# Convolution stage of a decoder: the order of one turn held by edges, and squares summed on ScalarE

## The chip, the cores and the metric

The kernel runs on one core of a Trainium2 chip, as one launch. A core has a matrix engine (TensorE, PE in the profile; its weight loads are listed as PEld), three engines for elementwise work (VectorE or DVE, ScalarE or ACT, GpSimd or POOL) and a queue engine that issues transfers (SyncE or SP). Each engine works off its own list of instructions in order; an instruction that needs another engine's result waits on a semaphore, and all that stands behind it on the same engine waits with it. The metric is the device time of the launch in microseconds, and lower is better.

## What is computed

The reference is a decoder of four layers with twelve sublayers on 128 x 64 tokens of width 128, each followed by a layer norm. Only the ninth sublayer is touched, `_L2_ffn_ref`; what matters of it:

```
xc  = silu(pointwise(depthwise_conv3(x)))
x1  = x + xc
logits = x1 @ router_w.T + router_b
top_v, top_i = top_k(logits, 2);  top_w = softmax(top_v)
rw  = sum(one_hot(top_i, 8) * top_w)               # 8 experts
ye  = silu(einsum('bsd,eod->bseo', x1, expert_w) + expert_b)
combined = einsum('bse,bseo->bso', rw, ye)
h   = rmsnorm(x1 + combined @ out_w.T + out_b) * norm_w
ff  = gelu(h @ ff_down_w.T + ff_down_b)
out = h + ff @ ff_up_w.T + ff_up_b
x   = layernorm(x + out)
```

## The kernel before

All tokens stay on chip as 16 chunks `X[c]` of 512 tokens (4 tiles of 128 tokens by 128 features). The function `ffn_conv` goes through them in 8 turns of two chunks. Three generators and helpers make up a turn:

- `begin(i)` prepares turn i. For each chunk of the pair it transposes (L1932, `xT_ps`, copied to `xp`), convolves with three matmuls (L1943, `pw_ps`), takes the SiLU on ScalarE (L1945) and adds on GpSimd to give `x1T` in `box` (L1946). Then the router's logits for both chunks (L1951, `lg`), copied to `lgT`, transposed back (L1957, `lgr`), and the top-two weights in 18 small VectorE operations (L1959 and L428 to L475, with one in between on ScalarE, L470). It yields six times: xT, xT, pw, pw, lg, route.
- `units(i, n, t)` is one of eight units of a turn, here g0 to g7. All eight experts for 128 tokens: four matmuls into two PSUM banks (L1975, and L1977 for the bias), two SiLUs on ScalarE (L1979), the product with the routing weights on VectorE (L1980, 128x1024), and three halving adds: L1981 (on GpSimd for odd t, on VectorE for even t), L1982 and L1983 on GpSimd. The results lie in a ring of four buffers.
- `end(i)` finishes turn i: transposes the sums (L1990, `sT`, copied at L1991), multiplies by `out_w` and adds `x1` (L1999 and L2000, `z`), adds the bias on VectorE (L2002, `acc`), squares on ScalarE (L2004), sums on VectorE (L2005), and takes the root in `norm` (L2008, then `rsqrt`, L347 to L352, eleven small VectorE operations in one chain). The same root also serves the layer norm of the turn before: `ln_stats` (L373, L375, L376) gives its variance, and `ln_apply` a scale `lns` (L382) and eight ScalarE operations (L385) that write `X`. Then eight scalings of `acc` (L2016), the transposes `oT` (L332, copied at L339), `with_bias` on GpSimd (L401) and an add of `acc` (L2022), both into `xb`; the small ffn down (L2027, `dn`), its Gelu on ScalarE (L2029, with a table load before it and one after), up (L2035, `u`) and the add (L2037). The yields are: sT, sT, z, z, norm, scaled, oT, oT, dn, u.

The loop at the end of `ffn_conv` says between which units each piece is issued. A scheduler may still move instructions on an engine past each other where nothing forbids it. PSUM has 5 banks for units and others (`wide`) and 3 for all the rest (`bank`); the `r` tiles, which hold `xb`, have 3 buffers, `acc` has 2.

In this version `end` of a turn is spread over the whole of the next one, and its last two pieces (dn, u) are taken in the turn after that (`tail`). `tc.issue_after(ins)` gives every instruction traced in its block an edge behind `ins` if it is on the same engine as `ins`: it fixes an order, and adds no wait.

Of the kernel before, what the change touches and what calls it, by code (L numbers as in the profile page):

```python
# [16 lines left out]
AF = mybir.ActivationFunctionType  # L17
ALU = mybir.AluOpType
AX = mybir.AxisListType
# [6 lines left out]
TPC = 4  # L26
# [214 lines left out]
def tile_decoder(ctx: ExitStack, tc: tile.TileContext, a, out):  # L241
# [9 lines left out]
    mm = nc.tensor.matmul  # L251
# [60 lines left out]
    def row(n):  # L312
        return rows[:, _ROW_AT[n][0] : _ROW_AT[n][1]]
# [54 lines left out]
    def ln_stats(r, v):  # L368

        st = sm.tile([P, TPC, 6], F32, tag="lnst", name="lnst")  # L370
        mv = sm.tile([P, TPC, 2], F32, tag="lnmv", name="lnmv")
        for t in range(TPC):
            V.bn_stats(st[:, t, :], r[:, t, :])  # L373
        for t in range(TPC):
            V.bn_aggr(mv[:, t, :], st[:, t, :])  # L375
        V.tensor_scalar(v, mv[:, :, 1], LN_EPS, None, ALU.add)  # L376
        return mv

    def ln_apply(c, r, mv, y, store=False, on_act=False, on_dve=False):
        if on_act:  # L380
            s = sm.tile([P, TPC], F32, tag="lns", name="lns")
            last = V.scalar_tensor_tensor(s, mv[:, :, 0], -1.0, y, ALU.mult, ALU.mult)  # L382
        for t in range(TPC):
            if on_act:
                A.activation(X[c][:, t, :], r[:, t, :], AF.Identity, bias=s[:, t : t + 1], scale=y[:, t : t + 1])  # L385
            else:
                (V if on_dve else G).tensor_scalar(X[c][:, t, :], r[:, t, :], mv[:, t, 0:1], y[:, t : t + 1], ALU.subtract, ALU.mult)  # L387
        if store:
            nc.sync.dma_start(out=out_v[c], in_=X[c])
        return last if on_act else None  # L390
# [766 lines left out]
    def rows32(t, g):  # L1157
        return t[32 * g : 32 * g + 32]
# [731 lines left out]
    def ffn_conv():  # L1890
# [77 lines left out]
        def units(i, n, t):  # L1968

            s = S_[i]  # L1970
            y = ring[count[0] % 4]
            count[0] += 1
            ps = [wide("ye_ps") for _ in range(2)]
            for k in range(2):
                mm(ps[k].rearrange("p (e d) -> p e d", e=4), s["x1T"][n][:, t * P : (t + 1) * P], w[0][:, 4 * k : 4 * k + 4, :], start=True, stop=False, skip_group_check=True)  # L1975
            for k in range(2):
                mm(ps[k], rows32(ones, k), rows32(be, k)[:, k * 512 : (k + 1) * 512], start=False, stop=True, skip_group_check=True)  # L1977
            for k in range(2):
                s["silu"] = A.activation(y[:, 4 * k : 4 * k + 4, :], ps[k].rearrange("p (e d) -> p e d", e=4), AF.Silu)  # L1979
            V.tensor_tensor(y, y, s["w"][:, n * TPC + t, :, None].to_broadcast([P, E8, D]), ALU.mult)  # L1980
            (G if t % 2 else V).tensor_tensor(y[:, :4], y[:, :4], y[:, 4:], ALU.add)  # L1981
            G.tensor_tensor(y[:, :2], y[:, :2], y[:, 2:4], ALU.add)  # L1982
            G.tensor_tensor(s["sum"][n][:, t * D : (t + 1) * D], y[:, 0], y[:, 1], ALU.add)  # L1983

        def end(i):
            s = S_[i]
            for n in pair:
                ps = bank("sT_ps")
                for t in range(TPC):
                    nc.tensor.transpose(ps[:, t * P : (t + 1) * P], s["sum"][n][:, t * P : (t + 1) * P], ident)  # L1990
                A.copy(s["sumT"][n], ps)  # L1991
                yield
            v = sm.tile([P, 2, 2, TPC], F32, tag="cv", name="cv")
            acc = []
            for n in pair:
                z = bank("z")
                for t in range(TPC):
                    q = slice(t * P, (t + 1) * P)
                    mm(z[:, q], s["x1T"][n][:, q], ident, start=True, stop=False)  # L1999
                    mm(z[:, q], s["sumT"][n][:, q], w[1][:, 1, :], start=False, stop=True)  # L2000
                h = work("o", (P, TPC, D), "acc")
                V.tensor_tensor(h, z.rearrange("p (t d) -> p t d", t=TPC), row("outb")[:, None, :].to_broadcast([P, TPC, D]), ALU.add)  # L2002
                sq_ = work("ye", (P, TPC, D), "sq")
                A.activation(sq_, h, AF.Square)  # L2004
                V.tensor_reduce(v[:, 0, n], sq_, AX.X, ALU.add)  # L2005
                acc.append(h)
                yield
            V.tensor_scalar(v[:, 0], v[:, 0], 1.0 / D, 1e-6, ALU.mult, ALU.add)  # L2008

            y = norm(v, i - 1, S_[i - 1] if i else None)  # L2010
            yield
            hT, base = [], []
            for n in pair:
                h = acc[n]
                for t in range(TPC):
                    V.scalar_tensor_tensor(h[:, t, :], h[:, t, :], y[:, 0, n, t : t + 1], row("normw"), ALU.mult, ALU.mult)  # L2016
            yield
            for n in pair:
                h = acc[n]
                hT.append(transposed(h, "oT"))  # L2020
                b = with_bias(2 * i + n, "upb")
                G.tensor_tensor(b, b, h, ALU.add)  # L2022
                base.append(b)
                yield
            ps = bank("dn_ps")
            for n in pair:
                mm(ps[32 * n : 32 * n + 32, :], col("downw"), hT[n], start=True, stop=True)  # L2027
            g = work("xT", (64, 512), "g32")
            A.activation(g, ps[:64, :], AF.Gelu, bias=col("downb")[:64])  # L2029
            yield  # L2030
            us = [bank("u") for _ in pair]
            for t in range(TPC):
                q = slice(t * P, (t + 1) * P)
                for n in pair:
                    mm(us[n][:, q], rows32(g, n)[:, q], rows32(w[1], n)[:, 2, :], start=True, stop=True)  # L2035
            for n in pair:
                V.tensor_tensor(base[n], us[n].rearrange("p (t d) -> p t d", t=TPC), base[n], ALU.add)  # L2037
            s["r"] = base
            yield

        def norm(v, i, s):
            if s is None:
                G.memset(v[:, 1], 1.0)
            else:
                mv = [ln_stats(s["r"][n], v[:, 1, n]) for n in pair]
            y = rsqrt(v.rearrange("p a n t -> p (a n t)"), 4 * TPC, "rms").rearrange("p (a n t) -> p a n t", a=2, n=2)
            if s is not None:
                for n in pair:
                    ln_apply(2 * i + n, s["r"][n], mv[n], y[:, 1, n], on_act=True)
            return y  # L2050

        def take(it, n=1):
            for _ in range(n):
                next(it, None)
# [1 line left out]
        none = iter(())  # L2056
        first = begin(0)
        take(first, 7)
        tail = none
        for i in range(turns):  # L2060
            b = begin(i + 1) if i + 1 < turns else none
            e = end(i - 1) if i else none
            for g in range(8):
                units(i, g // TPC, g % TPC)
                if g == 0:
                    take(tail)
                    take(b, 2)
                elif g == 1:
                    take(tail)
                    take(e, 2)  # L2070
                elif g == 2:
                    take(b, 2)
                elif g == 3:
                    take(e, 3)
                elif g == 4:
                    take(e)
                elif g == 5:
                    take(b)
                elif g == 6:
                    take(b)  # L2080
                elif g == 7:
                    take(e, 2)
            tail = e
        take(tail, 2)
# [4 lines left out]
        norm(v, turns - 1, S_[turns - 1])  # L2089
        return S_[turns - 1]["silu"].ins  # L2090


# [130 lines left out]
```

## Time and profile before

| | us |
|---|---|
| median of 9 runs | 3190.74 |
| lowest, highest | 3177.69, 3201.59 |
| profiled execution | 3201.5 |
| its span | 3199.7 |
| the convolution's work lies at about | 2134 to 2490 |

In the stretch from 2305 to 2345 us, about one turn, the busy times are: PE 36.15, VectorE 33.63, ScalarE 18.72, GpSimd 24.66 of 40 us, at a mean granted TensorE clock of 0.91; transfers are near nothing. Between 2145 and 2465 us, mean durations of one instruction: L1980 1.313 us (least 1.184), L1979 0.600, L1981 on GpSimd 1.379 and on VectorE 0.769, L1982 0.860, L1983 0.659, L2016 0.605, L1946 1.250, L401 1.368, L2022 1.775, L2004 0.629, L2005 0.682. A mean well above the least duration means that the instruction was held up while it ran.

How to read the views: the chain of work gives the work that ended last, followed back in time; the waits give, for each pair, who stood still until whom; the timeline lists instructions by start, with their length, and in brackets the idle time of the engine before them and what ended it; "x8" at the end means that eight were merged into one line. The windows give the busy time of each engine within a stretch.

### The profile page before, as it was taken

Reading aid. Unit: us, or ns where it says so; the run is one execution under the profiler, and the core shown is the slowest. Engines: PE = TensorE matmul, PEld = TensorE weight load, DVE = VectorE, ACT = ScalarE, POOL = GpSimd, SP = SyncE. Lnnn points to the kernel's source line nnn. Section 1 sums busy time; section 2 is a strip of 40 time slices with the busy share of each in tenths; the row PEclk is TensorE's granted clock in tenths of the full one; section 3 lists DMA queues with packets and bytes.
Section 4 is the critical chain, followed back from the end, with each engine's and each line's share of the span. In section 5 each row is a group of like instructions: output and inputs, shape, how many; then the busy total and the mean of one; then the engine's idle time right before and its main releaser. Section 6 shows DMA issues by size and latency. Waiting matters only on the chain. (4 is left out here: it accounts for less than half of the span.)

```text
span 3199.7 us, 110578 instructions
## 1 busy us (share of the span) xinstructions
PE 2809.2 (88%) x46690; PEld 2058.0 (64%) x46690; DVE 2023.5 (63%) x7300; ACT 1620.9 (51%) x3150; POOL 1534.4 (48%) x1543
## 2 busy tenths in 40 slices
PE   5899989989898999997799989999997679998993
PEld 3789856656666677865577767764433347766882
DVE  3732469667777666553376656667889876674355
ACT  2444468845444555332366555544454556654453
POOL 3566566144554444334277445556665223344344
PEclk9999989999998999898899989989998889997996
DMA  4578821000002000014511000000000000011783
GB/s 127 151 205 259 240 59 43 12 2 3 3 3 63 11 4 4 6 32 114 154 18 18 4 5 4 4 11 1 1 1 10 1 6 18 19 33 54 216 249 112
DMA packets 191633, 182.22 MB, mean 57 GB/s; under 512 B 30176, under 2 KB 166624, under 8 KB 191136
## 3 DMA queue, kind: packets, MB, share of 16 engines
q1 hardware_dynamic: 160688, 136.66, 14.7%
q0 software_dynamic: 20224, 32.28, 4.3%
q8 instruction: 366, 6.00, 0.8%
q10 hardware_dynamic: 10224, 6.22, 0.7%
q14 instruction: 131, 1.07, 0.1%
HBM read 132.34 MB, written 42.73 MB: 55 GB/s over the span
## 5 line engine op out<-in xcount | busy, mean ns | idle before, releaser
L1243 DVE TENSOR_REDUCE m<-s_ps 128x8 f32<-128x512 f32 x640 | 397.2, 682 | 133.1 <-PE s_ps L1602 47.2
L1292 ACT ACTIVATE e<-t_ps 128x512 f32<-128x512 f32 x640 | 329.9, 602 | 158.0 <-PE t_ps L1285 157.4
L1310 PE MATMUL av_ps<-vx,e 128*64 128x18 f32 (+1 forms) x10240 | 344.7, 217 | 8.3 <-issue 7.3
L1310 PEld LDWEIGHTS av_ps<-vx,e 128*64 128x64 f32 x10240 | 325.7, 141 | 29.5 <-issue 22.1
L792 ACT ACTIVATE hT<-h_ps,aux 128x256 f32<-128x256 f32 x496 | 206.8, 469 | 228.4 <-PE h_ps L790 119.3
L1187 POOL TENSOR_SCALAR eb<-qT,small 128x512 f32<-128x512 f32 x80 | 131.4, 1643 | 344.8 <-ACT qT L972 149.7
L1273 PE MATMUL t_ps<-eb,kT 32*64 32x128 f32 x10240 | 282.7, 286 | 6.8 <-DVE m L1243 2.3
L825 POOL DMA_INDIRECT got<-l_rout,fat x192 | 191.9, 1000 | 179.1 <-DVE r L835 70.3
L790 PE MATMUL h_ps<-ebT,rw 128*128 128x256 f32 x992 | 244.6, 391 | 19.0 <-DVE ebT L778 11.0
L803 PEld LDWEIGHTS yg<-rw,hT 128*128 128x128 f32 x1984 | 242.8, 193 | 6.6
L1273 PEld LDWEIGHTS t_ps<-eb,kT 32*64 32x64 f32 x10240 | 199.6, 132 | 73.3 <-DVE m L1243 25.7
L803 PE MATMUL yg<-rw,hT 128*128 128x128 f32 x1984 | 243.0, 276 | 0.0
L1235 PE MATMUL s_ps<-eb,qT 32*64 32x256 f32 x5120 | 219.5, 400 | 18.4 <-POOL eb L1187 9.4
L387 POOL TENSOR_SCALAR x<-xb,lnmv,ln_y 128x128 f32<-128x128 f32 x200 | 157.0, 797 | 160.8 <-DVE ln_y L352 160.8
L1315 DVE RECIPROCAL rc<-av_ps 128x32 f32<-128x32 f32 (+1 forms) x192 | 61.5, 320 | 241.5 <-PE av_ps L1310 241.2
L765 POOL DMA_INDIRECT aux<-in_x_dram,rat x156 | 159.7, 1024 | 113.3 <-PE h_ps L790 48.8
L790 PEld LDWEIGHTS h_ps<-ebT,rw 128*128 128x128 f32 x992 | 183.9, 196 | 45.0 <-DVE ebT L778 15.8
L804 DVE TENSOR_TENSOR yo<-yg,aux 128x256 f32<-128x256 f32 x124 | 52.3, 422 | 243.4 <-PE yg L803 243.2
L1185 ACT ACTIVATE eb<-qT,small 128x512 f32<-128x512 f32 x160 | 106.8, 715 | 128.7 <-POOL qT L1412 123.9
L1187 POOL TENSOR_SCALAR eb<-kT,small 128x512 f32<-128x512 f32 x80 | 144.8, 1810 | 21.5 <-ACT kT L972 11.5
L1235 PEld LDWEIGHTS s_ps<-eb,qT 32*64 32x64 f32 x5120 | 113.9, 134 | 60.8 <-issue 14.5
L1975 PE MATMUL ye_ps<-w_l2f,box 128*128 128x512 f32 x256 | 136.2, 651 | 0.0
(519 smaller groups left out, 6367.4 us busy)
## 6 DMA issues: line engine op xcount, KB each, us to landing
rw<-in_l0w_dram SPq DMA_DIRECT2D x78, 512.0 KB
rw<-in_l3w_dram SPq DMA_DIRECT2D x46, 512.0 KB
l_rout<-yo SPq DMA_DIRECT2D x124, 128.0 KB
aux<-xd SPq DMA_DIRECT2D x46, 128.0 KB
aux<-in_l0b_dram SPq DMA_DIRECT2D x78, 66.0 KB
xd<-vx SPq DMA_DIRECT2D x5, 1024.0 KB
plan<-xr ACTq DMA_DIRECT2D x18, 256.0 KB
x<-in_x_dram SPq DMA_DIRECT2D x16, 256.0 KB
```

Source lines behind the costliest of these rows:

```text
L387: (V if on_dve else G).tensor_scalar(X[c][:, t, :], r[:, t, :], mv[:, t, 0:1], y[:, t : t + 1], ALU.subtract, ALU.mult)
L765: s.gather = G.indirect_dma_start(out=eb[:, i, :], out_offset=None, in_=x[:, :], in_offset=bass.IndirectOffsetOnAxis(ap=at[:, i : i + 1], ...
L790: s.pe = mm(ps[:, j * GR : (j + 1) * GR], w1[:, (k + j) * P : (k + j + 1) * P], ebT, start=True, stop=True)
L792: s.act_ins = A.activation(hT[k + j], ps[:, j * GR : (j + 1) * GR], s.act, bias=v[:, k + j : k + j + 1])
L803: s.pe = mm(y[:, i * P : (i + 1) * P], hT[k][:, i * P : (i + 1) * P], w2[:, k, :], start=(k == 0), stop=(k == FK - 1))
L825: s.gather = G.indirect_dma_start(out=got[i][k][:, t, :], out_offset=None, in_=s.rout[b][:, :], in_offset=bass.IndirectOffsetOnAxis(ap=at[ ...
L1187: ins = (G if h == 2 else V).tensor_scalar(dst, x, mine, None, ALU.mult)
L1235: mm(ps[g][j * S : (j + 1) * S, u * 256 : (u + 1) * 256].rearrange("p (h k) -> p h k", h=4), rows32(s["q"], g)[:, b], rows32(s["eb"], g)[: ...
L1243: last = V.tensor_reduce(s["m"][:, g, 2 * hf : 2 * hf + 2, :].rearrange("p t h -> p (t h)"), ps[g].rearrange("p (n k) -> p n k", k=S), AX. ...
L1273: mm(ps[g][i * S : (i + 1) * S].rearrange("p (a u j q) -> p a u j q", u=2, a=2, j=2)[:, :, u, j, :], rows32(s["k"], g)[:, b], rows32(s["eb ...
L1292: last = A.activation(e[:, g, :], ps[g], AF.Exp, scale=scale)
L1310: mm(av[j * S : (j + 1) * S, 8 * (u - u0) + n, :], ev[:, n // 2, n % 2, u, j, :], vx[:, 2 * (2 * hf + u) + j, n, :], start=True, stop=True,)
```

## The change

Seven things are edited, all in `ffn_conv`:

1. `end`: the square of 128x512 (L2004) and the sum of its rows on VectorE (L2005) become four ScalarE squares of 128x128, each of which also gives the sum of its rows (`accum_out`).
2. `end`: `ln_stats` of the turn before is issued behind each half of `z`, and no longer in `norm`.
3. `end`: the root (`roots`), the eight scalings and then `ln_apply` (`applied`) are one piece, with no yield between them.
4. The loop: the units behind the scaling get an edge behind the last scaling, so that on VectorE no product may come between the root and the scalings.
5. The loop: all pieces get an edge behind the last matmul of the unit before them.
6. The loop: z and root come behind g2 (they were behind g3), the second half of `begin`'s convolution behind g3 (it was behind g2), oT behind g5 (g7), dn behind g6 (g0 of the next turn), u behind g7 (g1 of the next turn).
7. `tail` is gone.

```diff
         def end(i):
...
-                A.activation(sq_, h, AF.Square)
-                V.tensor_reduce(v[:, 0, n], sq_, AX.X, ALU.add)
+                for t in range(TPC):
+                    A.activation(sq_[:, t, :], h[:, t, :], AF.Square, accum_out=v[:, 0, n, t : t + 1])
                 acc.append(h)
+                if i:
+                    mv.append(ln_stats(S_[i - 1]["r"][n], v[:, 1, n]))
                 yield
             V.tensor_scalar(v[:, 0], v[:, 0], 1.0 / D, 1e-6, ALU.mult, ALU.add)
-
-            y = norm(v, i - 1, S_[i - 1] if i else None)
-            yield
-            hT, base = [], []
+            if not i:
+                G.memset(v[:, 1], 1.0)
+            y = roots(v)
             for n in pair:
                 h = acc[n]
                 for t in range(TPC):
-                    V.scalar_tensor_tensor(h[:, t, :], h[:, t, :], y[:, 0, n, t : t + 1], row("normw"), ALU.mult, ALU.mult)
+                    last = V.scalar_tensor_tensor(h[:, t, :], h[:, t, :], y[:, 0, n, t : t + 1], row("normw"), ALU.mult, ALU.mult)
+            s["scaled"] = last.ins
+            if i:
+                applied(i - 1, mv, y)
             yield
...
             for g in range(8):
-                units(i, g // TPC, g % TPC)
...
+                with tc.issue_after(scaled) if scaled else nullcontext():
+                    pe = units(i, g // TPC, g % TPC)
+                with tc.issue_after(pe):
+                    if g == 0:
+                        take(b, 2)
+                    elif g == 1:
+                        take(e, 2)
+                    elif g == 2:
+                        take(e, 3)
+                        scaled = S_[i - 1]["scaled"] if i else None
+                    elif g == 3:
+                        take(b, 2)
+                    elif g == 5:
+                        take(e, 2)
+                        take(b)
+                    elif g == 6:
+                        take(e)
+                        take(b)
+                    elif g == 7:
+                        take(e)
```

The two programs can be built and their lists of instructions compared, engine by engine. For a steady turn of the changed one (turns 2 to 6) the lists are these, with the line numbers of the kernel before:

```
TensorE  g0, xT, g1, sT, g2, z, z, g3, pw, pw, g4, g5, oT, oT, lg, g6, dn, lgr, g7, u
ScalarE  SiLU g2, squares (4, 4), SiLU g3, box (first), L385 x8, box (second),
         SiLU g4, SiLU g5, oT copies, lgT copy, SiLU g6, table load, Gelu, table load, SiLU g7
VectorE  L1980 g2, acc (first), L1981 g2, acc (second), L2008, root (11), scaling (8), lns (2),
         L1980 g3, L1980 g4, L1981 g4, L1980 g5, L1980 g6, L1959, L1981 g6, 11 of routing,
         L2037, 1 of routing, L1980 g7, 2 of routing, L2037, the other 3 with statistics,
         L1980 g0, L1981 g0, statistics, L1980 g1, statistics
GpSimd   L1982 and L1983 g2, L2022 (first), L1946 (first), L1981 g3, L401, L1982 g3,
         L2022 (second), L1983 g3, L401 (for the next turn), L1946 (second),
         then L1982 and L1983 of g4, L1981 to L1983 of g5, and so on to g1
```

In the kernel before, the same piece of GpSimd's list reads: L1946 (first), L1946 (second), then the adds of three units, L2022 (first), L401, L2022 (second), L401 (for the next turn); on TensorE `oT` stands between the first matmuls of the next turn's g0 and g1, and on VectorE products and routing stand between the root's operations. Outside of the convolution stage and its border with the next one, the lists are the same.

More of the change, by code (lines that the diff above doesn't have):

```diff
@@ L1976, in units @@
             for k in range(2):
-                mm(ps[k], rows32(ones, k), rows32(be, k)[:, k * 512 : (k + 1) * 512], start=False, stop=True, skip_group_check=True)
+                pe = mm(ps[k], rows32(ones, k), rows32(be, k)[:, k * 512 : (k + 1) * 512], start=False, stop=True, skip_group_check=True)
             for k in range(2):
@@ L1983, in units @@
             G.tensor_tensor(s["sum"][n][:, t * D : (t + 1) * D], y[:, 0], y[:, 1], ALU.add)
+            return pe.ins
         def end(i):
@@ L1993, in end @@
             v = sm.tile([P, 2, 2, TPC], F32, tag="cv", name="cv")
-            acc = []
+            acc, mv = [], []
             for n in pair:
@@ L2015, in end @@
                 for t in range(TPC):
-                    V.scalar_tensor_tensor(h[:, t, :], h[:, t, :], y[:, 0, n, t : t + 1], row("normw"), ALU.mult, ALU.mult)
+                    last = V.scalar_tensor_tensor(h[:, t, :], h[:, t, :], y[:, 0, n, t : t + 1], row("normw"), ALU.mult, ALU.mult)
+            s["scaled"] = last.ins
+            if i:
+                applied(i - 1, mv, y)
             yield
+            hT, base = [], []
             for n in pair:
@@ L2039, in end, with roots, applied @@
             yield
[L2041 to L2050, printed above, removed]
+        def roots(v):
+            return rsqrt(v.rearrange("p a n t -> p (a n t)"), 4 * TPC, "rms").rearrange("p (a n t) -> p a n t", a=2, n=2)
+        def applied(i, mv, y):
+            for n in pair:
+                ln_apply(2 * i + n, S_[i]["r"][n], mv[n], y[:, 1, n], on_act=True)
         def take(it, n=1):
@@ L2058, in ffn_conv @@
         take(first, 7)
-        tail = none
+        scaled = None
         for i in range(turns):
@@ L2063, in ffn_conv @@
             for g in range(8):
-                units(i, g // TPC, g % TPC)
[L2065 to L2084, printed above, removed]
+                with tc.issue_after(scaled) if scaled else nullcontext():
[18 more added lines that the diff above has]
+                        take(e)
         for _ in end(turns - 1):
@@ L2088, in ffn_conv @@
         G.memset(v[:, 0], 1.0)
-        norm(v, turns - 1, S_[turns - 1])
+        mv = [ln_stats(S_[turns - 1]["r"][n], v[:, 1, n]) for n in pair]
+        applied(turns - 1, mv, roots(v))
         return S_[turns - 1]["silu"].ins
```

## The prediction

> **What bounds the kernel now.** The granted clock and engine shares of the whole span say little here: the change touches one stage. I read first the chain of work that ended last between 2120 and 2520 us, where the convolution stage lies (start, length, engine, tile, line):
>
> ```profile
> 2305.79 5.42 PE pw_ps L1943 x12
> ...
> 2319.98 0.64 ACT sq L2004
> ...
> 2331.69 4.32 DVE acc L2016 x8
> ...
> 2347.96 5.42 PE pw_ps L1943 x12
> ```
>
> The same piece of work comes back every 42.2 us: one turn. The second square of a turn stands in this chain at 2195.62, 2235.64, 2277.80, 2319.98, 2362.15 and 2404.67; the timeline has the seventh at 2439.85. These six periods, 244.2 us, are what the change can alter most; I measure all by this mark (the second `acc` ends just before it).
>
> Second, the waits between 2145 and 2465 us (who waited for whom: total us, times, longest):
>
> ```profile
> PEld oT_ps L332 <- DVE acc L2016: 38.5, 31, 7.1
> PE oT_ps L332 <- DVE acc L2016: 25.6, 17, 6.8
> ACT x L385 <- DVE lns L382: 17.0, 6, 4.5
> PEld lg_ps L1951 <- POOL box L1946: 8.8, 7, 4.3
> ```
>
> TensorE stands before the transposes `oT` until VectorE has scaled: about 3.7 us a turn. The last row is small now: `lg` seldom waits for GpSimd.
>
> Third, the timeline of one turn, 2327.5 to 2349 us. Here VectorE and GpSimd hold each other up:
>
> ```profile
> 2331.61 4.40 DVE L2016 SCALAR_TENSOR_TENSOR acc<-acc,rms_y,rows 128x128 f32<-128x128 f32 x8
> 2331.65 3.19 ACT L385 ACTIVATE x<-xb,lns,rms_y 128x128 f32<-128x128 f32 x8 [2.44 <-DVE lns L382]
> ...
> 2333.02 1.31 POOL L2022 TENSOR_TENSOR xb<-xb,acc 128x512 f32<-128x512 f32 x1 [0.75 <-DVE acc L2016]
> 2334.28 1.31 POOL L401 TENSOR_TENSOR xb<-x,rows 128x512 f32<-128x512 f32 x1
> ...
> 2336.07 1.21 DVE L1980 TENSOR_TENSOR units<-units,route 128x1024 f32<-128x1024 f32 x1
> ...
> 2336.15 2.25 POOL L2022 TENSOR_TENSOR xb<-xb,acc 128x512 f32<-128x512 f32 x1 [0.55 <-DVE route L436]
> ```
>
> The eight scalings need 4.40 us; one alone is 0.34 (the line's minimum is 0.336). The second L2022, caught behind a product L1980, takes 2.25 us where the first took 1.31. So a VectorE operation on two SBUF tiles and a GpSimd operation take turns, and whichever is queued waits out the other.
>
> Fourth, the busy time in 2-us windows (length, PE, PEld, DVE, ACT, POOL, granted clock):
>
> ```profile
> 2333.80:2335.80 2.00, 0.74 (x2) 0.18 (x2) 2.00 (x3) 1.51 (x4) 1.80 (x2) 0.60 0.04 8
> 2335.80:2337.80 2.00, 2.00 (x4) 0.86 (x5) 2.00 (x4) 0.00 (x0) 1.65 (x1) 0.50 0.00 0
> 2337.80:2339.80 2.00, 2.00 (x4) 0.53 (x2) 1.93 (x4) 0.58 (x1) 2.00 (x3) 0.50 0.00 0
> 2339.80:2341.80 2.00, 2.00 (x9) 0.60 (x9) 1.90 (x5) 0.90 (x3) 1.84 (x3) 0.69 0.00 0
> ```
>
> After the stall the clock is at half for some 7 us; with 0.60, 0.50, 0.50 and 0.69 that is 3.4 us of lost matmul time. The stall is thus paid twice, and removing it should bring 5 us a turn, if nothing replaces it.
>
> **The change, part by part, on a steady turn.** Let 0 be the end of the second `acc`. I follow the built order of each engine, in the line numbers of the kernel before, and put measured durations on it.
>
> *Squares.* Two 128x512 squares (0.63) and two VectorE reductions (0.68 each) go; eight 128x128 squares with a sum come. No row shows a sum taken by ScalarE. Bounds for one: 0.17 (L1816, a 128x128 ACTIVATE, 0.275, less the 0.11 by which two SiLUs of 0.597 overlap) and 0.48 (L385, 128x128 with two pointers). I take 0.35, nearer L385, whose pitch is 3.19/8 = 0.40. The last four are on the path: 1.4 us, 0.05 hand-over. The Trainium skill, "ScalarE: Activation LUTs", section "What ACT_TABLE_LOAD costs", gives 186 ns + 0.833 ns an element less about 93 of overlap, which as an estimate is 0.2 each, and the turn 0.6 shorter; it states no price for the sum, and no run here shows one.
>
> *Root and scaling unbroken.* Now they are spread from 2321.4 to 2336.0, 14.6 us, because products and routing lie between. Unbroken, the last turn of this profile shows their price: L347 at 2476.48 to the last L352 at 2478.73 is 2.25 us for 11 operations. Scaling:
>
> ```profile
> 2478.92 3.23 DVE L2016 SCALAR_TENSOR_TENSOR acc<-acc,rms_y,rows 128x128 f32<-128x128 f32 x8
> ```
>
> that is 3.23 beside one GpSimd operation; 4.40 beside three. In the new order two (L2022, L1946) are ready by then: 3.8. With L2008 (0.2) and two `lns` (0.25): 1.45 + 0.2 + 2.3 + 3.8 + 0.25 = 8.0 us. `oT` is then ready before TensorE, which has 13 us of work from `z` to there (g3, `pw` 5.3, g4, g5, at 2.24 a unit, plus `oT` 1.0). The old stall is gone.
>
> *What is queued behind it.* All products from g3 on now stand behind the scaling. On GpSimd the order is: L2022, L1946 (first half), then L1981 of g3, L401, L1982, L2022, L1983, L401, and only then L1946 for the second half, on which `lg` waits; and on TensorE `lg` stands before g6. On ScalarE the eight L385 (3.2 us) wait for `lns`, and behind them stand the second `box` (0.69) and the SiLUs of g4 and g5, so g4's product can't begin before 8.0 + 3.2 + 0.7 + 1.1 = 13 us. GpSimd: product g3 done at 9.25; then 1.27 + 1.26 + 0.73 + 1.30 + 0.46 + 1.26 + 1.19 = 7.5, hand-overs 0.3. VectorE's L1980, L1981, L1980 of g4 and g5 (3.1) arrive in that time and take turns; less 0.15 of overlap each, 2.7. So the second `lg` starts at 9.25 + 7.8 + 2.7 = 19.75 us. TensorE has been there since about 12: a stall of 7 us in place of the 3.7.
>
> *From `lg` on.* `lg` 0.86, g6 1.92, 0.48 to ScalarE, two SiLUs 1.08, 0.05: 4.4 us to the product of g6. After such a stall the clock is at half; bounds for this stretch 0 and 2.8 (all of it); I take 2.5 by the windows above. The skill's "TensorE: Matmul & The Clock Gate", Part 1, states that one busy window of 3.4 us restores full rate, which as an estimate would cost 1.7 instead; the rows above show it at half for longer. Product g6 at 26.65.
>
> VectorE's own queue from there to the next second `acc`: five L1980 at 1.21, three L1981 at 0.61, L1959 0.2, 17 routing operations at 0.25 (their pitch at 2145), two L2037 1.2, eight L373 1.7, eight L375 0.65, two L376 0.3, two `acc` 1.3: 17.5 us bare. GpSimd's 7.3 us for g6, g7, g0 and g1 take turns with it; some 4 show. Bounds: 1.5 (they fall under the operations that don't contend) and 6.9 (the factor of the present turn, from 2336.0 to 2354.1: 18.1 us for 13.0 bare; 17.5 x 0.39). With 4: 21.5. **Period: 26.65 + 21.5 = 48.1 us** against 42.2.
>
> *Ends.* In the first turn that ends another, there are no L385, L401 or statistics yet: so GpSimd's list there is L2022 twice, product g3's L1981 and L1982, then the second L1946: scaled 8.7, L2022 10.0, product g3 11.25, L1981 12.5, one L1980 13.7, L1982 14.4, L1981 15.1, L1946 16.3; with 4.4 + 0.8 (a shorter stall, clock mostly up) + 21.5 the period is 43 (41 to 45) against 40.0. The first mark comes 5.3 us earlier, as `pw` now follows `z`. The small ffn inside its turn removes, at the end, a wait of 4.09 us (`sT` for L2037, at 2467.69), but the last product, now behind the scaling, comes at about 24.6 after the mark instead of 17.4; the sums then take 2.6, so `sT` follows at 27.4 against 27.9: nothing. Cover for that is GpSimd's sum; were it gone, 4 us would be won. No DMA is moved.
>
> Sum: -5.3 + 43 + 5 x 48.1 - 244.2 = **+34 us**. The profiled execution took 3201.5 us (span 3199.7, 1.8 around it), so 3235.5; it lies 10.8 above the median of 3190.74, so on the scale of medians **3225**.
>
> **Rivals.**
> *The stall goes for good* (faster). If GpSimd and VectorE hardly met and the clock stayed up: `lg` at 7.4 + 1.25 + 7.8 = 16.5, product g6 at 20.9, plus 17.5: 38.4 a turn. -5.3 + 39 + 192 - 244.2 = -18.5: 3172; a quarter of the contention and clock loss counted above gives 3185. For it: the waits of `oT` for `acc` do vanish. Against: the L2022 of 2.25 us.
> *TensorE sets the pace* (about even). VectorE keeps up (contention 1.5) and only `lg` stalls: 19.75 + 0.86 + 2.24 + the rest of the turn's matmuls 16.7 + 2.5 + 1.1 for `acc`, 43.2. -5.3 + 41 + 216 - 244.2 = +7.5: 3198. Decides if VectorE reaches the second `acc` when `z` ends.
> *More contention* (slower). 6.9 in place of 4, squares 0.48 each, scaling 4.4: 52.1 a turn, 45 for the first, +56: 3247.
> *The order isn't what it says*: the built orders exclude it, but if ScalarE's sum were a long operation (1 us each), the period grows by 2.6, to 3238.
>
> **How the numbers follow.** About 0.3%, 9.6 us, is what a measurement of this kernel can tell from no change. Forecast 3225 (its own range 3205 to 3245): 0.62; stall gone: 0.13; TensorE's pace: 0.15, of which 0.08 within 0.3%, 0.03 faster and 0.04 slower; more contention and the long sum: 0.10. Faster 0.13 + 0.03 = 0.16, same 0.08, slower 0.62 + 0.04 + 0.10 = 0.76. The range reaches down to a quarter of the contention, 3184, and up to the case of more contention, 3247; about 2 in 10 lie outside.
>
> **What would show it.** Right: the wait of `oT` for `acc` near nothing; a wait of `lg` for L1946 of 5 to 8 us a turn; L347 to the last L352 within 2.5 us; marks about 48 us apart; granted clock at half after `lg`. Wrong: `lg` waiting under 3 us, or marks under 42 us apart: then GpSimd's queue was ready sooner than I count, and the forecast falls with it.

## The result, and the profile after

The changed kernel takes **3211.81 us** (median of 20 runs, 3191.76 to 3224.84); the kernel before, run beside it, 3189.99 (62 runs). The ratio is 1.0073, with a 95% interval of 1.0058 to 1.0087: slower by 19 to 28 us. The profiled execution took 3215.5 us (span 3213.8).

Line numbers are now those of the changed kernel: `acc` L2003, squares L2006, L2011 (was L2008), scaling L2018, the add of `acc` into `xb` L2028, `dn` L2033, Gelu L2035, `u` L2041 and L2043; up to L1983 nothing moved. A turn is measured from mark to mark, the mark being the end of its second `acc`. I cut the stage at three points: the first `pw` weight load, the seventh mark, and the last weight load of `kva`, near the end of the next stage (`attn_scan`), which begins under the convolution's last turns.

| us | before | after | difference | predicted |
|---|---|---|---|---|
| first `pw` to first mark | 64.2 | 57.0 | -7.2 | -5.3 |
| first period | 40.0 | 41.7 | +1.7 | +3 |
| four steady periods | 169.0 | 177.8 | +8.8 | +23.4 |
| sixth period | 35.7 | 44.1 | +8.4 | +12.4 |
| seventh mark to last `kva` | 153.4 | 160.0 | +6.6 | 0 |
| sum | 462.3 | 480.6 | +18.3 | +34 |

The first and the sixth period's rows belong together: `pw` now follows `z`, so every mark but the last ones comes a `pw` earlier, and the kernel before has no `pw` left in its sixth period. Together they make +1.2, and the sixth turn's own loss is in it. A steady turn takes 44.4 us against 42.2. The chain of work that ended last, in the changed kernel, from one mark (2322.82) on (start, length, engine, tile, line):

```profile
2326.94 3.86 DVE acc L2018 x7
2330.94 1.15 DVE units L1980
2332.16 1.27 POOL units L1981
2333.43 1.22 POOL xb L401
...
2336.51 1.45 POOL box L1983
2337.96 1.67 POOL xb L401
2339.63 2.12 POOL box L1946
2341.79 1.92 PE lg_ps L1951 x2
2343.71 3.22 PE ye_ps L1975 x4
...
2348.54 1.23 DVE units L1980
```

Before, this part of the chain was scaling and transposes; now it leads through GpSimd's whole list, add by add, to the second L1946, and only then to `lg` and g6. The waits between 2145 and 2465 us, one row of the kernel before, then the changed kernel's (who waited for whom: total us, times, longest):

```profile
DVE units L1980 <- ACT units L1979: 21.2, 14, 4.1
```

```profile
DVE units L1980 <- ACT units L1979: 68.0, 12, 8.1
...
PE lg_ps L1951 <- POOL box L1946: 40.0, 8, 6.0
...
PE oT_ps L332 <- DVE acc L2018: 1.1, 2, 0.9
```

TensorE's old wait (25.6 us, `oT` for the scalings) is nearly gone (1.1); a wait of 40.0 for GpSimd stands in its place, and VectorE, which waited 21.2 us for SiLUs before, now waits 68.0. The timeline of VectorE in one turn shows where:

```profile
2324.16 0.17 DVE L2011 TENSOR_SCALAR cv<-cv 128x8 f32<-128x8 f32 x1 [1.34 <-ACT sq L2006]
...
2326.67 4.13 DVE L2018 SCALAR_TENSOR_TENSOR acc<-acc,rms_y,rows 128x128 f32<-128x128 f32 x8
...
2335.73 1.92 DVE L1980 TENSOR_TENSOR units<-units,route 128x1024 f32<-128x1024 f32 x1 [3.65 <-ACT units L1979]
...
2348.54 1.23 DVE L1980 TENSOR_TENSOR units<-units,route 128x1024 f32<-128x1024 f32 x1 [7.83 <-ACT units L1979]
```

Three gaps in a turn: 1.34 us for the squares, 3.65 for g4's SiLUs and 7.83 for g6's. In between it is busy without a pause. So the account of a turn is VectorE's: busy time and gaps. The windows view gives it, for one turn of the kernel before and then of the changed one (length, busy time of PE, PEld, DVE, ACT, POOL with instructions, granted clock):

```profile
2319.46:2361.62 42.16, 38.38 (x145) 17.30 (x144) 35.22 (x76) 20.85 (x41) 25.84 (x28) 0.92 0.00 0
```

```profile
2322.82:2367.25 44.43, 36.02 (x145) 16.73 (x144) 30.85 (x74) 22.17 (x55) 25.63 (x29) 0.88 0.00 1
```

VectorE's busy time falls by 4.4 us (35.22 to 30.85), but it stands still for 13.6 us in place of 6.9. The second outweighs the first by 2.3 us a turn.

### The profile page after: what moved, and what is told of

Same layout as the page of the kernel before. It is cut to its first block, busy times and chain, and to the rows that moved or that the text cites. A ratio compares the mean times of both kernels' runs of the same rounds, so it can differ in the third digit from the quotient of the medians.

```text
span 3213.8 us, 110706 instructions
## 1 busy us (share of the span) xinstructions
PE 2790.3 (87%) x46690; PEld 2047.6 (64%) x46690; DVE 1996.5 (62%) x7284; ACT 1634.4 (51%) x3264; POOL 1539.7 (48%) x1543
## 5 line engine op out<-in xcount | busy, mean ns | idle before, releaser
L1310 PE MATMUL av_ps<-vx,e 128*64 128x18 f32 (+1 forms) x10240 | 337.5, 215 | 9.2 <-issue 8.4
L1310 PEld LDWEIGHTS av_ps<-vx,e 128*64 128x64 f32 x10240 | 318.9, 139 | 29.8 <-issue 22.2
L1273 PEld LDWEIGHTS t_ps<-eb,kT 32*64 32x64 f32 x10240 | 198.9, 132 | 73.3 <-DVE m L1243 25.6
L765 POOL DMA_INDIRECT aux<-in_x_dram,rat x156 | 159.9, 1025 | 117.3 <-PE h_ps L790 51.7
L1980 DVE TENSOR_TENSOR units<-units,route 128x1024 f32<-128x1024 f32 x64 | 93.5, 1467 | 68.3 <-ACT units L1979 68.0
```

The lines of the kernel that those rows point to most:

```text
L765: s.gather = G.indirect_dma_start(out=eb[:, i, :], out_offset=None, in_=x[:, :], in_offset=bass.IndirectOffsetOnAxis(ap=at[:, i : i + 1], ...
L1273: mm(ps[g][i * S : (i + 1) * S].rearrange("p (a u j q) -> p a u j q", u=2, a=2, j=2)[:, :, u, j, :], rows32(s["k"], g)[:, b], rows32(s["eb ...
L1310: mm(av[j * S : (j + 1) * S, 8 * (u - u0) + n, :], ev[:, n // 2, n % 2, u, j, :], vx[:, 2 * (2 * hf + u) + j, n, :], start=True, stop=True,)
```

## Experiments

Each row below is one kernel; the times are from its profiled execution, the ratio is to the kernel before, run beside it on the same chip (the kernel before took 3317 us beside e1 and 3186 us beside e11, so only ratios are compared). Where one order is changed, the builder may move other instructions too; what it moved is told with each.

| run | period (mean of the second to fifth), us | first `pw` to 7th mark | 7th mark to last `kva` | ratio, 95% interval |
|---|---|---|---|---|
| before | 42.2 | 308.9 | 153.4 | 1 |
| after | 44.4 | 320.6 | 160.0 | 1.0073 (1.0058 to 1.0087) |
| e1 GpSimd's order | 39.2 | 293.4 | 159.8 | 0.9958 (0.9931 to 0.9985) |
| e2 ScalarE's order | 40.6 | 302.4 | 160.1 | 1.0011 (0.9988 to 1.0035) |
| e3 both | 40.8 | 299.6 | 156.6 | 0.9984 (0.9957 to 1.0010) |
| e4 no edge | 40.5 | 300.0 | 158.7 | 0.9994 (0.9964 to 1.0024) |
| e5 L385 behind Gelu | 44.5 | 315.4 | 146.5 | 1.0000 (0.9973 to 1.0026) |
| e6 last turn | 39.3 | 291.6 | 152.8 | 0.9973 (0.9947 to 0.9999) |
| e7 sums on VectorE | 40.4 | 299.8 | 162.1 | 1.0003 (0.9976 to 1.0031) |
| e8 before, sums on ScalarE | 43.4 | 312.1 | 150.8 | 1.0036 (1.0017 to 1.0055) |
| e9 L385 behind copies | 40.7 | 302.7 | 156.1 | 0.9974 (0.9955 to 0.9993) |
| e10 L385 split | 39.8 | 295.5 | 156.3 | 0.9965 (0.9948 to 0.9981) |
| e11 as e6 | 39.2 | 293.6 | 155.7 | 0.9971 (0.9954 to 0.9987) |
| e12 two adds fewer | 37.4 | 280.8 | 156.8 | 0.9937 (0.9907 to 0.9966) |

A profile is one execution. e6 and e11 are the same kernel twice: from the first `pw` to the first mark they take 54.0 and 56.8 us, from there to the seventh mark 237.6 and 236.7, and from that to the last `kva` 152.8 and 155.7. So the periods can be compared closely, and a difference of 3 us in the first or the last stretch says little.

### e1: the second `x1T` add ahead of the bias adds

The theory to test: GpSimd's order alone makes `lg` late.

```diff
+                s["x1"] = G.tensor_tensor(...x1T...).ins
...
-                b = with_bias(2 * i + n, "upb")
-                G.tensor_tensor(b, b, h, ALU.add)
+                with tc.issue_after(S_[i + 2]["x1"]) if i + 2 < turns else nullcontext():
+                    b = with_bias(2 * i + n, "upb")
+                    G.tensor_tensor(b, b, h, ALU.add)
```

> GpSimd takes the second x1T add (L1946) ahead of both bias adds and both adds of the scaled tile; nothing else moves. Theory (GpSimd's list alone keeps lg waiting): the second lg starts at 13.3 us after the mark (second box done 12.0, add 1.2) instead of 19.0, product g6 at about 20, the stretch to the next mark stays 18.7, period 38.7 instead of 44.4; five steady turns give -28 and the first -3: about 3181 us, ratio to before 0.997. Rival (contention: the four adds now fall beside VectorE's products and routing): stretch 21.5 to 23, period 41.5 to 43, 3195 to 3204. Rival (VectorE alone sets the pace): no gain, 3212.

VectorE's, ScalarE's and TensorE's lists stay as they were; only GpSimd's changes. The period falls from 44.4 to 39.2 us. The timeline of e1, from its mark at 2406.34 (GpSimd, then VectorE):

```profile
2417.15 1.17 POOL L1946 TENSOR_TENSOR box<-xp,box 128x512 f32<-128x512 f32 x1
2418.29 3.93 POOL L401 TENSOR_TENSOR xb<-x,rows 128x512 f32<-128x512 f32 x2
2422.18 4.45 POOL L2029 TENSOR_TENSOR xb<-xb,acc 128x512 f32<-128x512 f32 x2
...
2418.14 1.27 DVE L1980 TENSOR_TENSOR units<-units,route 128x1024 f32<-128x1024 f32 x1 [3.65 <-ACT units L1979]
2419.45 1.64 DVE L1981 TENSOR_TENSOR units<-units 128x512 f32<-128x512 f32 x1
2421.01 4.50 DVE L1980 TENSOR_TENSOR units<-units,route 128x1024 f32<-128x1024 f32 x2
```

L1946 is done 12.0 us after the mark (18.9 in the changed kernel), and the gap of 7.83 us is gone. The product of g6 ends 19.2 us after the mark in place of 26.95, 7.8 us sooner. But the four adds now lie beside products: two L1980 take 4.50 us together, where two undisturbed ones take 2.4 (e.g. 2.35 at 2462.83 in the changed kernel), and from the end of g6's product to the next mark it is 20.0 us in place of 17.5. So 7.8 is won and 2.5 given back: both the theory and the first rival hold in part. VectorE's busy time says the same, 33.38 against 30.85:

```profile
2406.34:2445.47 39.13, 35.68 (x146) 17.02 (x144) 33.38 (x74) 21.93 (x55) 26.91 (x29) 0.96 0.00 1
```

### e12: two GpSimd adds fewer

The disputed cost by itself: e1 with `with_bias` left out, `b = X[c] + h`, so that the bias of the small ffn is missing from its result.

```diff
-                    b = with_bias(2 * i + n, "upb")
-                    G.tensor_tensor(b, b, h, ALU.add)
+                    b = work("r", (P, TPC, D), "xb")
+                    G.tensor_tensor(b, X[2 * i + n], h, ALU.add)
```

> GpSimd's order, and the two bias adds (L401) of a turn left out, so that the small ffn's bias is missing in the result; VectorE, ScalarE and TensorE keep their lists, GpSimd has two adds of 1.22 us fewer. Theory (a VectorE operation on SBUF and a GpSimd operation take turns, so each GpSimd add queued beside VectorE's products lengthens VectorE's work by about its own time): period 39.2 less 2 to 2.5, 36.7 to 37.2, VectorE busy 34.1 to 32 in a turn. Rival (the products are long for another reason): 39.2. Rival (the other adds slide under the same products and half comes back): 38.

```profile
2300.67:2338.09 37.42, 34.20 (x145) 16.34 (x144) 31.67 (x74) 21.94 (x55) 24.36 (x27) 1.00 0.00 1
```

VectorE does the same 74 instructions in 31.67 us in place of 33.38, with the same gaps (1.34 and 3.65); the period falls by 1.7. Two adds of 1.22 us cost VectorE 1.7 us, 0.7 of their own time; expected were 2 to 2.5. Over the four steady turns the busy time falls from 33.46 to 31.66 us: 0.55 of it in the products, 0.81 in the halving adds, 0.49 in the routing, and nothing in root and scaling together. "Take turns" is right, the full price is not. A reason can be read from e1's trace: in its steady turns a product takes between 1.21 and 2.29 us, but L2003, L2044 and L373, which read one tile of SBUF, keep to 0.68, 0.68 and 0.28 us beside GpSimd's adds, so what of an add falls beside those costs nothing. The Trainium skill, "SBUF — State Buffer", section "Who interferes with whom", says that a VectorE instruction with two SBUF inputs contends with a GpSimd instruction that reads SBUF, and that one with at most one SBUF input, outside VectorE's two-port modes, does not; these durations agree.

### e2 and e3: L385 behind the SiLUs of g4 and g5

The other thing that comes late is g4's product (gap of 3.65 us), since its SiLUs stand behind eight L385 on ScalarE.

```diff
-            if i:
-                applied(i - 1, mv, y)
             yield
+            if i:
+                with tc.issue_after(S_[min(i + 1, turns - 1)]["silu"].ins):
+                    applied(i - 1, mv, y)
+            yield
...
                     elif g == 5:
-                        take(e, 2)
+                        take(e, 3)
```

> ScalarE takes the eight L385 behind the second box and the SiLUs of g4 and g5; the builder then also sets the second x1T add ahead of the bias adds on GpSimd. Theory: second lg at 12.6 us after the mark (product g3 9.25, A1 1.3, A2 0.75, add 1.2), and the products of g4 and g5 follow g3 at once (VectorE idle there 0 instead of 3.65); period 37.5 to 38.5, about 3178 us, ratio 0.996. Rival (when g4 and g5 come does not matter, only lg): the same as the run with GpSimd's order alone, 38.7, 3181. Rival (L385 late holds up statistics or buffers): over 41, 3195 or more.

> Both orders together. Theory: as with ScalarE's order alone, since the second x1T add is already early there; 3175 to 3180 us. Rival (bias adds behind the x1T add meet VectorE's products): 3185 to 3195.

e2 is this edit alone (the builder then also sets the second L1946 ahead of L401), e3 has e1's as well. Both beat the changed kernel, 40.6 and 40.8 us, but neither comes near 38, and e3's period is longer than e1's. The timeline of e3, mark at 2386.09:

```profile
2398.04 3.18 ACT L385 ACTIVATE x<-xb,lns,rms_y 128x128 f32<-128x128 f32 x8
2401.12 1.05 ACT L339 COPY oT<-oT_ps 128x512 f32<-128x512 f32 x2
...
2404.30 0.23 DVE L1959 TENSOR_TENSOR route<-lgr_ps,rows 128x64 f32<-128x64 f32 x1 [3.85 <-PE lgr_ps L1957]
```

L385 now stands in front of the `oT` copies; `dn` waits for those, `lgr` stands behind `dn` on TensorE, and L1959, which the builder put ahead of g6's product, waits 3.85 us (4.72 in e2). The gap has moved, not shrunk. Neither theory held; nearest comes e2's last rival (L385 late, over 41 us), but what L385 holds up is `dn` and `lgr`, not statistics or buffers.

### e4: no edge behind the scaling

```diff
-                with tc.issue_after(scaled) if scaled else nullcontext():
+                with nullcontext():
                     pe = units(i, g // TPC, g % TPC)
```

> Products are not held behind the scaling: the edge is left out, one product now stands inside the root, the second box stands ahead of L385 and the second x1T add ahead of the unit adds. Theory (the edge is what makes lg late): root and scaling end 1.3 us later, second lg at 10 to 13 us, oT waits under 1 us, period 38 to 40, 3178 to 3188 us. Rival (scaling early is what pays): oT waits again 3 us a turn and the time is above the changed kernel's, 3215 to 3230.

One product now lies inside the root, and the builder puts the second box ahead of L385 on ScalarE and both L1946 ahead of the bias adds. The scalings take 5.00 us in place of 4.13 and end 11.5 us after the mark in place of 8.0; `oT` waits 7.3 us between the first mark and the seventh, 1.2 us a turn. Yet the period is 40.5, a little above what was expected, and the time at the upper end of it: with the edge left out, and L1946 early, 4 us a turn are back. This does not show that the edge costs them. e1 has L1946 early too, keeps the edge, and its period is 1.3 us shorter than e4's (whose second box also stands elsewhere). So the loss lies in GpSimd's order that came with the edge, not in scaling early.

### e5, e9 and e10: other places for L385

All with e1's order; e9 and e10 also with the last turn of e6, below. e5 puts the eight behind the Gelu, e9 behind the `oT` copies; e10 puts four behind the copies and four behind the Gelu, and holds the statistics of the next turn behind g7's product.

```diff
-            A.activation(g, ps[:64, :], AF.Gelu, bias=col("downb")[:64])
+            gelu = A.activation(g, ps[:64, :], AF.Gelu, bias=col("downb")[:64])
+            if i:
+                with tc.issue_after(gelu.ins):
+                    applied(i - 1, mv, y)
...
+            if i:
+                with tc.issue_after(last_copy[0]):
+                    applied(i - 1, mv, y)
             ps = bank("dn_ps")
```

> GpSimd's order as in the run with GpSimd's order alone, and on ScalarE the second box and the SiLUs of g4 and g5 first, the eight L385 only behind the Gelu, in front of g7's SiLUs. Theory (with GpSimd's order VectorE sets the pace: of its 39.2 us it stands idle 1.34 before L2011 and 3.65 before the product of g4): the 3.65 shrink to about 1.6, period 37 to 37.5, 12 us less than with GpSimd's order alone, ratio to before 0.991 to 0.993. Rival (a late ScalarE chain takes the place, as where L385 stood in front of the oT copies: VectorE idle 3.85 before L1959): period 39 to 41, ratio 0.996 to 0.999.

> GpSimd's order, the last turn's old end, and on ScalarE the second box and the SiLUs of g4 and g5 first, then the oT copies, then the eight L385, in front of g6's SiLUs. Theory (VectorE sets the pace; idle 1.34 before L2011 and 3.65 before g4's product with GpSimd's order alone): 3.65 shrink to 1.7, but g6's SiLUs come up to 3 us later and VectorE waits 1 to 2 there: period 38.2 to 39.5, stage within 6 us of 444. Rival (Gelu and with it u, the statistics and xT come late, as where L385 stood behind the Gelu): 42 to 44.

> As the run with L385 behind the copies, but four L385 there and four behind the Gelu, and VectorE's statistics held behind the product of g7. Theory: neither g6's SiLUs nor g7's product come late; VectorE idle 1.34 plus 1.7 plus under 1; period 37.2 to 38.2, stage 434 to 440, ratio to before 0.991 to 0.993. Rival (the builder's other shifts give it back): 39 to 40, ratio 0.994 to 0.996.

None beats e1's 39.2: 44.5, 40.7 and 39.8. e5 lies above its theory and its rival, e9 (stage 458.8 us) above its theory, e10 in its rival's range. In e5 g7's SiLUs come behind L385, and the builder set its product behind all routing and statistics, 28.6 us after the mark (26.3 in e1). Its sums on GpSimd come late, `sT` waits for them, and with it g2 (VectorE, TensorE, VectorE; mark at 2403.70):

```profile
2432.32 2.35 DVE L1980 TENSOR_TENSOR units<-units,route 128x1024 f32<-128x1024 f32 x2
...
2438.37 0.47 PE L1991 MATMUL sT_ps<-ident,box 128*128 128x128 f32 x1 [4.10 <-POOL box L1983]
...
2444.01 1.23 DVE L1980 TENSOR_TENSOR units<-units,route 128x1024 f32<-128x1024 f32 x1 [4.99 <-ACT units L1979]
```

e10 is the telling one, for there nothing on ScalarE is late any more (mark at 2304.74; in this kernel L1981 are the SiLUs and L1982 the products):

```profile
2314.71 1.36 DVE L1982 TENSOR_TENSOR units<-units,route 128x1024 f32<-128x1024 f32 x1 [1.73 <-ACT units L1981]
...
2321.73 1.58 DVE L1982 TENSOR_TENSOR units<-units,route 128x1024 f32<-128x1024 f32 x1 [2.67 <-ACT units L1981]
...
2320.54 1.08 ACT L1981 ACTIVATE units<-ye_ps 128x512 f32<-128x512 f32 x2 [0.55 <-PE ye_ps L1979]
```

VectorE's gaps are 1.34, 1.73 and 2.67, no less in sum than e1's 1.34 and 3.65, and the SiLUs behind the last one waited for TensorE. TensorE has no gap from the mark until then: `pw` 5.4 us, three units, `oT`, `lg`, up to 2320.4, 15.7 us after the mark. So with L385 out of the way VectorE waits for matmuls in the first half of a turn; e5 has the same two gaps, 1.73 and 2.67, there. e10's mean holds one turn of 41.2 us; its other three take 39.2 to 39.4, e1's period.

### e6 and e11: the border with the next stage

The prediction had put the border at nothing; it measured +6.6 us. VectorE's timeline between the last two marks of the kernel before, then of the changed kernel (L2132 and L2134 are the sums with which `attn_scan` begins; the L2002 shown is the second and last `acc` of the last turn, the L2003 the first):

```profile
2457.09 0.67 DVE L2132 TENSOR_REDUCE lnv<-sq 128x4 f32<-128x512 f32 x1
...
2466.07 0.68 DVE L2132 TENSOR_REDUCE lnv<-sq 128x4 f32<-128x512 f32 x1
...
2473.59 0.68 DVE L2002 TENSOR_TENSOR acc<-z,rows 128x512 f32<-128x512 f32 x1
```

```profile
2483.45 0.69 DVE L2003 TENSOR_TENSOR acc<-z,rows 128x512 f32<-128x512 f32 x1 [7.95 <-PE z L2001]
...
2485.31 0.65 DVE L2134 TENSOR_REDUCE lnv<-sq 128x4 f32<-128x512 f32 x1
```

Before, four of these statistics were done 7.5 us ahead of the last mark. Now VectorE stands still for 7.95 us in front of `acc` and begins them only behind it: the last SiLU, which `attn_scan` is held behind, comes after the Gelu of the same turn, and the builder listed the statistics later. ScalarE had the squares for two of them ready at 2474.4, 9 us before that `acc`; as far as the profile shows, only VectorE's list kept the sums back. The test: in the last turn alone, the small ffn again behind all units, and no edge.

```diff
-                        scaled = S_[i - 1]["scaled"] if i else None
+                        scaled = S_[i - 1]["scaled"] if i and i + 1 < turns else None
+                    elif i + 1 == turns:
+                        continue
...
+        take(e, 4)
         for _ in end(turns - 1):
```

> GpSimd's order, and in the last turn alone the small ffn of the turn before again behind all units and no edge behind the scaling, so that VectorE's list has the statistics of three chunks of attn_scan ahead of the last acc. Theory (the border cost 8.6 us since those statistics came behind): from the eighth mark to the last kva 119 to 122 us instead of 127.8, first kva steps 5.4 to 6.5 us apart again; the ratio 0.002 below that of GpSimd's order alone, 0.9935. Rival (border set by the sums and transposes of the last units): still 126 to 128, ratio 0.996.

> The kernel with GpSimd's order and the last turn's old end once more, beside the two others on one chip: stage 444 us, 18 less than before, so the ratio 0.994 to 0.996 if the rest of the kernel is unchanged; 0.997 again would say that some of the 18 are lost elsewhere.

```profile
2527.87 1.26 DVE L2138 TENSOR_REDUCE lnv<-sq 128x4 f32<-128x512 f32 x2
2535.05 0.68 DVE L2138 TENSOR_REDUCE lnv<-sq 128x4 f32<-128x512 f32 x1
2541.08 0.69 DVE L2003 TENSOR_TENSOR acc<-z,rows 128x512 f32<-128x512 f32 x1 [2.20 <-PE z L2001]
```

In e6 three statistics stand ahead of `acc` again, and from the eighth mark to the last `kva` it takes 117.3 us (expected 119 to 122; e1 127.8). The fourteen profiles divide the same way: where at least two sums stand ahead of the last turn's first `acc` (before, e5, e6, e8, e9, e11) this stretch takes 114 to 121 us, where none does (after, e1 to e4, e7, e10, e12) 126 to 129. e5 has them ahead without the edit, and in e10, which has the edit, they stand behind: it is their place that counts. A third of e6's gain is paid with a later eighth mark; from the seventh, it is 152.8 and 155.7 in e6 and e11, against 159.8 in e1 and 153.4 before. The stage as a whole, 444.4 and 449.3 us, is 13 to 18 us shorter than before. The times agree with less of it: e6 0.9973 where 0.9935 was expected, e11 0.9971, 9 us (4 to 15), where 0.994 to 0.996 was; where the rest goes was not found. And e1 without this edit is not told apart from e6 by the ratios. All three have their whole interval below 1: they beat both kernels.

### e7 and e8: what the sums on ScalarE are worth

e7 is e1 with the two squares of 128x512 and the two VectorE reductions of the kernel before; e8 is the kernel before with the accumulating squares, and nothing else.

```diff
-                for t in range(TPC):
-                    A.activation(sq_[:, t, :], h[:, t, :], AF.Square, accum_out=v[:, 0, n, t : t + 1])
+                A.activation(sq_, h, AF.Square)
+                V.tensor_reduce(v[:, 0, n], sq_, AX.X, ALU.add)
```

> GpSimd's order, with the squares as before: two 128x512 squares and two reductions on VectorE. Theory (VectorE sets the pace): two reductions of 0.66 more on it, and from the second acc to L2011 about 2.0 us with 0.6 of it covered; period 39.9 to 40.7 against 39.2, 6 to 10 us more in all, ratio 0.998 to 0.999. Rival (the eight accumulating squares are the dearer form): period 38.5 to 39, ratio 0.994.

> The kernel before with this part of the change alone: squares summed by ScalarE. Theory (worth it wherever VectorE is behind): 0.5 to 1.2 us a turn less, 3 to 8 us in all, ratio 0.9975 to 0.999. Rival (in that kernel the root is spread between products, and the squares are off the path): within 0.05%. Rival (1 us a sum): +10 us, ratio 1.003.

In e7 the period rises from 39.2 to 40.4, as expected (the ratio, 1.0003, is above the 0.998 to 0.999 that was): where VectorE sets the pace, the accumulating form is worth 1.1 us a turn. In the kernel before it brings nothing: the period rises to 43.4, and the ratio, 1.0036 (1.0017 to 1.0055), is above all that was expected but the one that took a sum for 1 us. A sum is not that long (0.30 us, below). One line of e8's timeline (mark at 2387.44):

```profile
2389.27 0.83 DVE L2008 TENSOR_SCALAR cv<-cv 128x8 f32<-128x8 f32 x1 [1.83 <-ACT sq L2005]
```

There the second four squares stand behind both boxes on ScalarE, as the single square did, so VectorE waits 1.83 us where it had waited 1.19 and reduced for 0.69, and gains nothing on the path. Why the next `pw` then starts 30.2 us after the mark in place of 28.5 was not separated: the builder also moved g0's SiLUs ahead of L470, and products and pieces of the root past each other on VectorE. So e8 is not the form alone. Its stage is only 0.7 us longer in all than before, but the execution profiled was its fastest, 20 us below its median; most of its +12 us (6 to 18) stays open.

## Why the prediction was right in kind and too large

*Right.* All of the first 26 us of a turn: L2011 stands idle 1.34 us (1.4 predicted for the last four squares), the root takes 2.26 (2.3), the scalings 4.13 (3.8), `lns` ends 8.1 us after the mark (8.0), g3's product at 9.26 (9.25). GpSimd's list holds the second `lg` until 18.97 (19.75), and from there to g6's product it is 6.75 us (6.9, with 2.5 for the clock). TensorE's stall there is 5.96 us (7). That the stall moves from `oT` to `lg` is shown by the waits, that GpSimd's order alone makes it by e1.

*The term that was mis-sized:* "GpSimd's 7.3 us for g6, g7, g0 and g1 take turns with it; some 4 show". From g6's product to the next mark it took 18.7 us, not 21.5: 1.2 on top of the 17.5 us bare, below the lower bound of 1.5. With this and 0.9 us saved ahead of it the period is 44.4 instead of 48.1; over five turns that is 18 us, more than the whole error. e12 and e1 give the size: an add costs VectorE 0.7 of its time when it lies beside products, halving adds and routing, and in e1, where bias adds and the adds of g4 and g5 run on into this stretch, it is 2.5 us longer. In the changed kernel those adds ran at 2333 to 2346 us, while VectorE stood idle for 3.65 and 7.83 us. What is left of GpSimd's work in the stretch follows each product and falls beside short operations and statistics; that this is why it costs so little is read from the timeline, and no run tested it. The marks 48 us apart, named as a sign of being right, did not come. The prediction sized the contention between a lower bound and the factor of the kernel before; but in that kernel the four adds lie in the busy part, and here the stall had already cleared them away.

*The step that was wrong:* "nothing" for the last turn. The prediction followed the last `sT` (done 28.1 us after the seventh mark; 27.4 predicted) and stopped there. That the two numbers agree is luck: the last product was not late (done 18.9 us after the mark, 24.6 predicted), but GpSimd then worked without a pause from 8.4 to 26.7 us after the mark, the bias adds among its work, before the last sum was there. The statistics of the next stage had been hidden in that turn; they lost their cover, and 6.6 us show from the seventh mark to the last `kva`, of which e6 and e11 get 4 to 7 back. This error and the first have opposite signs, which is why the total, +22 us on the medians where 34 was predicted, lies nearer than its parts: that, too, is luck.

*A remark that doesn't add up:* "removing it should bring 5 us a turn". The two figures beside it, 3.7 and 3.4 us, make 7.1. It enters no sum, and no run removed the old stall alone; e1, with neither stall, is 3.0 us a turn below the kernel before.

*Not covered:* the stage explains 18.3 us, by one execution of each kernel, and two executions of one kernel differed by 5 us there (e6, e11); the time differs by 19 to 28.

## What to carry to other kernels

When a chain on one engine is made unbroken, read the lists of the other engines that are fed behind it: here the gain was real (e1 keeps 1.8 us a turn of VectorE's busy time, 35.2 to 33.4; the rest of the 4.4 was GpSimd's work falling into the gaps) and was lost because GpSimd had four adds that nobody waited for ahead of the one that TensorE waited for, and moving that one add forward turned a loss of 0.7% into a gain of 0.4% (0.15 to 0.7). A stall and a contention are not simply to be added: here, while VectorE stood still, GpSimd worked its queue off undisturbed. And at the end of a stage, look at what the next one had been doing in its gaps.

## What the runs showed of the hardware

A 128x128 square that also sums its rows is two records on ScalarE, an ACTIVATE of 0.29 us and a read of the accumulator of 0.19, which overlap: eight in a row come every 0.30 us, less than the 0.40 of L385 with its two pointers.

The eight scalings, unbroken, took 2.19 us in e12 with no GpSimd add beside them, 3.01 in the turn of e1 shown above with one, and 4.13 in the changed kernel with two.

The clock, in the windows of the changed kernel around the stall (columns as above; the granted clock is the third from the end):

```profile
2334.00:2336.00 2.00, 1.02 (x2) 0.14 (x2) 0.27 (x1) 2.00 (x5) 2.00 (x3) 1.00 0.00 0
2336.00:2338.00 2.00, 0.00 (x0) 0.00 (x0) 1.97 (x2) 1.55 (x4) 2.00 (x3) 0.52 0.00 0
...
2345.00:2346.00 1.00, 1.00 (x2) 0.33 (x1) 0.00 (x0) 0.00 (x0) 0.60 (x2) 0.50 0.09 16
2346.00:2347.00 1.00, 1.00 (x4) 0.09 (x2) 0.00 (x0) 0.00 (x0) 0.00 (x0) 0.84 0.00 0
```

After a gap of 2.05 us and one `lg`, it falls to half at 2336.1, just behind the start of the second gap, and stays there until 2346.3, 4.5 us after TensorE resumes at 2341.79; in the five steady stalls of this kernel it was 4.5 to 4.8. The Trainium skill, "TensorE: Matmul & The Clock Gate", Part 1, states that about 3.4 us of sustained work bring the full rate back, in windows that run freely; the stalls here took a microsecond longer, which such a window's start can make, and no run here tests it. With the stall gone, in the turn of e12 shown above, the clock is 1.00 throughout.
